# Attention's weighted sums as seven block products, run in 64-column halves of the matmul array

## The chip, the cores and the metric

One core of one Trainium2 chip runs the whole kernel. The metric is the device time of one execution in microseconds (us), lower is better. Engines are named as in the profile: PE (matrix products; PEld loads their stationary operand), DVE (vector), ACT (scalar), POOL (GpSimd) and SP, which only issues transfers (DMAs). ACT and POOL issue transfers too; such an issue takes its place in the engine's own order, so what is written behind it waits until it has been issued.

## The reference

A layer norm, 16-head attention over 2048 rows (head size 128) and a gated feed-forward with ternary weights, all added to x. The change concerns the line that sums `v` with the softmax weights; all of it is float32.

```python
xn = layernorm(x)                                    # x: 1 x 2048 x 256
q, k, v = heads(einsum('bsd,ed->bse', xn, Wqkv))     # 16 heads of 128
logits = einsum('bqhd,bkhd->bhqk', q, k) * 128 ** -0.5
w = softmax(logits)
out = einsum('bhqk,bkhd->bqhd', w, v)                # the weighted sums
x + einsum('bse,de->bsd', out.reshape(1, 2048, 2048), Wout) + ffn(xn)
```

## The kernel before

**Blocks and steps.** After a lead-in of about 100 us (layer norm, feed-forward, first projections) one loop runs over 64 blocks: 16 heads by 4 blocks of 512 queries. Block `n` has four steps, `t` = 0 to 3. A step computes the scores of one tile `v` of 128 queries against all 2048 keys, six tiles ahead of the weighted sums (`LEAD`, L52), and a quarter of the weighted sums of block `n`. So in step `(n, t)` PE works on the scores of tile `u + 6`, DVE turns tile `u + 4` (which is tile `t` of block `n + 1`) and PE sums block `n`.

**A step on each engine.** The loop stands under `tc.manual_schedule()` (L932): each engine runs its instructions in the order in which the code writes them.

- PE: four score products of 512 columns (L612), the first of two "side" products (`beside`; projections of later heads or the output projection, L166, L280 or L783), three or two weighted-sum products (L690), the second side product, the remaining one or two weighted-sum products. Some steps have a single side product or none. Every float32 product of 128 x 128 x 512 appears as two MATMUL records.
- DVE: the two maxima of the scores (L617), their negated maximum `nm` (L620), the sums that read the side products (L186 to L206, L304, L790), the inverses of the softmax sums at `t` = 2 (L660 to L663), the two transposes of an older tile (L680).
- ACT: two exponentials (L627) which need `nm`, then six of the sixteen transfers that exchange 32-row strips between partitions (`exchanged`, L646).
- SP: the other ten of those transfers. An exchange moves `p` into `part`; the transposes L680 then turn `part` into `pT`, with the keys on the partitions. `p` has buffers for two tiles, `part` too.
- POOL: small transfers (`put_away` L708, `spread` L672, the inverses L665, moves of the output sums L716 and L720, `v_exchanged` L311) and differences of operands for the side products (L138 to L141, L261 to L264, L723).

**Buffers in PSUM.** Three score buffers (`ps_s`), one buffer for the weighted sums (`ps_av`, one bank) and one for the side products (`ps_m`).

**Weighted sums.** `weighted(n, k)` adds the product of key tile `k` of `v` (128 keys x 128) and `pT` (128 keys x 512 queries) into one bank, 16 products for a block, four in each step. After the last one a single DVE instruction (L701) multiplies the bank with the inverse softmax sums, which `spread` has laid into `oT`, and `put_away` stores `oT` in DRAM at `t` = 0 of the next block. The last four blocks leave the inverse to a later line; the last block is summed in two halves of 256 columns behind the loop.

**Side products** already use a seven-product scheme for blocks of 2 x 2: differences of operands are formed on POOL, and DVE adds each product into the results that need it.

Of the kernel before, what the change touches and what calls it, by code (L numbers as in the profile page):

```python
# [19 lines left out]
def layernorm_attention_bitffn_kernel(  # L20
# [15 lines left out]
    P = 128  # L36
# [48 lines left out]

    banks = []

    def bank(shape, name: str):
# [63 lines left out]
    def fast_product(h: int, b: int, i: int, second: bool):  # L152

        c = b // 2 * 2
        wk, wq = (weights[h // G, i][:, :, bass.ts(h % G, D)] for i in "kq")
        w, t = ws[h], ts[c]
        x00, x10 = (xnT[:, d, bass.ts(c, QB)] for d in range(KC))
        x11 = xnT[:, 1, bass.ts(c + 1, QB)]
        lhs, rhs = {
            (0, 0): ((wk[:, 0], x00), (w[:, 1], t[:, 1])),  # L160
            (0, 1): ((w[:, 2], t[:, 2]), (wq[:, 1], t[:, 3])),
            (1, 0): ((w[:, 0], t[:, 0]), (w[:, 3], x11)),
            (1, 1): ((wk[:, 1], x10),),
        }[b % 2, i][second]
        pm = ps_m.tile([P, QB], F32, tag="m", name=f"pw{h}_{b}_{i}_{int(second)}")
        nc.tensor.matmul(pm, lhs, rhs, start=True, stop=True)  # L166
        return pm
# [100 lines left out]
    def fast_v_product(g: int, m: int, second: bool):  # L268
# [10 lines left out]
        pm = ps_m.tile([P, QB], F32, tag="m", name=f"pvw{g}_{half}_{m}_{int(second)}")  # L279
        nc.tensor.matmul(pm, lhs, rhs, start=True, stop=True)  # L280
        return pm
# [24 lines left out]
    def v_exchanged(h: int, half: int):  # L306

        v = v_half(h, half).rearrange("p k d -> p (k d)")
        for j in range(P // 32):
            for q in range(P // 32):  # L310
                nc.gpsimd.dma_start(  # L311
                    v_part[q // 2][bass.ts(j, 32), bass.ts(q % 2, S // 8)],
                    v[bass.ts(q, 32), bass.ts(j, S // 8)],
                )
# [284 lines left out]

    def scores(v: int, late=None):  # L600

# [7 lines left out]
        for i in range(2):  # L609
            s = ps_s.tile([P, HALF], F32, tag="s", name=f"s{v}_{i}")  # L610
            for j in range(HALF // QB):
                nc.tensor.matmul(  # L612
                    s[:, bass.ts(j, QB)], qTs[h, b][:, bass.ts(t, P)],
                    kTs[h][:, i * HALF + j * QB : i * HALF + (j + 1) * QB],
                    start=True, stop=True,
                )
            nc.vector.tensor_reduce(mx[:, i : i + 1], s, AX.X, ALU.max)  # L617
            halves.append(s)
        nm = small.tile([P, 1], F32, tag="nm", name=f"nm{v}")
# [49 lines left out]
    def spread(n: int):  # L669

        if n < NBK - NB:
            nc.gpsimd.dma_start(oT, rds[n % 2].rearrange("t p -> (t p)").partition_broadcast(P))  # L672
            rbs[n] = oT

    def transposed(v: int):
        n, t = divmod(v, TB)
        if t == 0:
            pTs[n] = apool.tile([P, TB, NQ, S // NQ], F32, tag="pT", name=f"pT{n}")
        for i, part in enumerate(parts.pop(v)):
            nc.vector.transpose(pTs[n][:, t, 2 * i : 2 * i + 2], part)  # L680

    def weighted(n: int, k: int, part=None):

        h, b = blocks[n]
        t0, t1 = (0, TB) if part is None else (part * TB // 2, (part + 1) * TB // 2)
        if k == 0:
            pool, tag = (ps_s, "s") if part == 0 else (ps_av, "av")
            avs[n] = pool.tile([P, QB], F32, tag=tag, name=f"av{n}_{t0}")
        av = avs[n][:, : (t1 - t0) * P]
        nc.tensor.matmul(  # L690
            av, v_tile(h)[:, v_place(h, k), :],
            pTs[n][:, t0:t1].rearrange("p t g (k q) -> p (t g) k q", q=32)[:, :, k, :],
            start=(k == 0), stop=(k == NKT - 1),
        )
        if k == NKT - 1:

            m = 1 if part == 1 else t1 - t0
            for t in range(t0, t1, m):
                o, a = oT[:, t * P : (t + m) * P], av[:, (t - t0) * P : (t - t0 + m) * P]
                if n < NBK - NB:  # L700
                    nc.vector.tensor_tensor(o, a, rbs[n][:, t * P : (t + m) * P], ALU.mult)  # L701
                else:
                    nc.vector.tensor_copy(o, a)

# [75 lines left out]
    def fast_o_product(g: int, m: int, second: bool):  # L780
        lhs, i, _ = o_parts(g, m)[second]
        pm = ps_m.tile([P, QB], F32, tag="m", name=f"pow{g}_{m}_{int(second)}")
        nc.tensor.matmul(pm, lhs, o3[:, i], start=True, stop=True)  # L783
        return pm
# [47 lines left out]
    def opened(b: int, u: int, pool=ps_m, tag: str = "m"):  # L832

        pm = pool.tile([P, 2, DM], F32, tag=tag, name=f"pp{b}_{u}")
        for j in range(2):
            nc.tensor.matmul(
                pm[:, j], o3[:, b % 2, bass.ts(2 * u + j, P)], weights[H // G - 1, "o"][:, 0, :],
                start=True, stop=True,
            )
# [3 lines left out]
    def projected(n: int, u: int, pool=ps_m, tag: str = "m"):  # L843
# [6 lines left out]
        for j in range(2):  # L850
            t = 2 * u + j
            if j % m == 0:
                pm = pool.tile([P, m, DM], F32, tag=tag, name=f"po{n}_{u}_{j}")
            pms.append(pm[:, j % m, :])
            nc.tensor.matmul(
                pms[j], oT[:, bass.ts(t, P)], weights[H // G - 1, "o"][:, 1, :],
                start=True, stop=True,
            )
# [26 lines left out]
    def between(n: int, t: int):  # L885
# [4 lines left out]
        how = {  # L890
            (5, 0): (v_exchanged, 0, 0), (5, 2): (v_transposed, 0, 0), (6, 1): (v_transposed, 1, 0),
            (7, 0): (v_exchanged, 0, 1), (7, 2): (v_transposed, 0, 1),
        }.get((i, t))
        if t == 0:
            if 0 < n <= last:
                put_away(n - 1)
        if t == 1:
# [16 lines left out]
        if t == 2:  # L914
            if i == GB - 1 and n < last:
                wo = weights[g, "o"]
                sums_of(wo[:, :, :P], wo[:, :, P:], f"wos{g}")
            if i in (5, 7) and g + 1 < H // G:
                v_exchanged((g + 1) * G + 1, i // 2 - 2)
        if t == 3:  # L920
            if i == NB - 1 and g + 1 < H // G:
# [10 lines left out]
    with tc.manual_schedule():  # L932
        for u in range(-LEAD, (NBK - 1) * TB):
# [24 lines left out]
            def beside():  # L958
# [4 lines left out]
                if seven:  # L963
                    pms.append(product(*hi, False))
                    read(*hi, False, pms[0])

            if more:
                scores(v, late=beside)

            if lead_in:  # L970
                for what, hg, i in first.get(v, ()):
                    {"q": q_piece, "k": k_piece, "v": v_piece}[what](hg, i)
                if v == 1:
                    front.close()
                    apool = ctx.enter_context(tc.tile_pool(name="apool", bufs=2))
                    oT = apool.tile([P, QB], F32, tag="oT", name="oT", bufs=1)
                    for c in range(0, NB, 2):
                        x_sums(c)
# [16 lines left out]
            twice = seven and twice  # L995
            ahead = KQ // 2 if first_of_pair else KQ - 1
            if u >= 0:
                for k in range(t * KQ, t * KQ + ahead):
                    weighted(n, k)
            if twice:  # L1000
# [12 lines left out]
            if u >= 0:  # L1013
                for k in range(t * KQ + ahead, (t + 1) * KQ):
                    weighted(n, k)
            if more and t == TB - 1:
# [4 lines left out]
            if t == 2 and n > NBK - NB:  # L1021
                projected(n - 1, 1)
            if u >= 0:
                between(n, t)

        n = NBK - 1
        for k in range(NKT):
            weighted(n, k, 0)
            if k in (KQ - 1, 3 * KQ - 1):
# [3 lines left out]
        for k in range(NKT):  # L1033
            weighted(n, k, 1)
            if k == KQ - 1:
# [41 lines left out]
```

## Time and profile before

| what | value |
|---|---|
| time, median of 3 runs | 2243.78 us (2242.69 to 2244.05) |
| span of the profiled execution | 2242.2 us |
| granted PE clock | 1.000 |
| DVE busy | 1772.0 us (79%) |
| ACT busy (its transfer issues not counted) | 652.4 us (29%) |
| POOL busy (its transfer issues counted) | 681.1 us (30%) |
| transfers of L646: SP, median of one issue | 2556, 589 ns |
| transfers of L646: ACT, median of one issue | 1540, 602 ns |
| DVE transpose of 128 x 256, L814 (nearest to a 256-column DVE sum) | 408 ns |
| ACT copy of 128 x 256 out of PSUM, L235 | 385 ns |
| POOL difference of 128 x 512 / of 128 x 128, L723 / L139 | 1271 / 452 ns |

A timeline line gives the start in us, the length in us, the engine, line and operation, the tiles written and read, the shape and how many instructions were merged; in brackets the idle time before it and what ended it. The engines ACTq and SPq are the issuing of transfers, which the profile doesn't count as busy. A row "x8" of MATMUL records stands for four float32 products. The end of a matmul record is modelled, so the pitch is read from the starts: eight score records started at 1020.28 us and the next record at 1023.71, 0.429 us a record or 0.857 us a product of 512 columns. With 256 columns 24 records of L690 took 5.34 us at the end of the kernel (2232.09 to 2237.43), 0.215 us a record.

### The profile page before, as it was taken

What the parts mean: (1) busy time and instruction counts of PE and PEld (TensorE: products, weight loads), DVE (VectorE), ACT (ScalarE), POOL (GpSimd) and SP (SyncE); (2) the same over time, 40 slices, a digit from 0 to 9 for tenths busy, and PEclk for the clock granted to TensorE, in tenths of its full rate; (3) what the DMA queues carried; (4) which work ended last, traced back from release to release, by engine and by line L of the source; (5) the groups of instructions that cost most, each with busy time, mean ns of one, the idle gap of its engine ahead of it and who ended that gap; (6) DMA issues with size and microseconds to landing.
All of it is one profiled execution on the core that took longest, in us unless ns stands there. A gap on an engine that the chain in (4) does not pass through costs nothing.

```text
span 2242.2 us, 24572 instructions
## 1 busy us (share of the span) xinstructions
PE 2230.5 (99%) x5434; PEld 1025.3 (46%) x5434; DVE 1772.0 (79%) x2329; ACT 652.4 (29%) x1138; POOL 681.1 (30%) x1223
## 2 busy tenths in 40 slices
PE   9999999999999999999999999999999999999999
PEld 6744444444444444444444444444444444444445
DVE  6577778888788878888788878788778887888876
ACT  5543222222222222222222222222222222222231
POOL 0021144231452223522234313332134221452442
PEclk9999999999999999999999999999999999999999
DMA  2166666775676666676666766667566676676775
GB/s 91 50 161 172 156 166 172 186 195 157 165 196 179 185 159 164 188 203 169 155 176 179 197 179 150 176 181 199 163 166 179 175 197 159 158 200 181 197 202 145
DMA packets 252515, 382.72 MB, mean 171 GB/s; under 512 B 86224, under 2 KB 90768, under 8 KB 252368
## 3 DMA queue, kind: packets, MB, share of 16 engines
q1 hardware_dynamic: 127664, 174.95, 30.3%
q10 hardware_dynamic: 74896, 101.94, 17.2%
q0 software_dynamic: 49808, 104.27, 16.6%
q8 instruction: 43, 0.70, 0.1%
q14 instruction: 104, 0.85, 0.1%
HBM read 62.98 MB, written 34.73 MB: 44 GB/s over the span
## 4 chain that ended last, share of the span: by engine, by line
PE 67%; DMA 16%; DVE 7%; SPq 5%; issue 2%; ACTq 2%; ACT 1%; DVEq 0%; POOL 0%
PE s L612 26%; PE av L690 25%; DMA part<-p 16%; PE pw L166 5%; SPq L646 5%; DVE pT L680 3%; PE pvw L280 3%; PE pow L783 3%; PE ph L495 2%; ACTq L646 2%; DVE mx L617 1%; PE pf L518 1%; ACT p L627 1%; DVE osums L790 1%; PE pv L229 1%
## 5 line engine op out<-in xcount | busy, mean ns | idle before, releaser
L627 ACT ACTIVATE p<-s,nm 128x1024 f32<-128x1024 f32 x512 | 566.1, 1110 | 1512.5 <-DMA part<-p 1269.5
L612 PE MATMUL s<-kT,qT 128*128 128x512 f32 x2048 | 922.5, 593 | 2.6 <-ACT p L627 2.4
L617 DVE TENSOR_REDUCE mx<-s 128x1 f32<-128x1024 f32 x512 | 623.6, 1221 | 353.5 <-PE s L612 353.3
L690 PE MATMUL av<-pT,v 128*128 128x512 f32 (+1 forms) x1952 | 888.4, 585 | 0.0
L680 DVE STREAM_TRANSPOSE pT<-part 128x1024 f32<-128x1024 f32 x512 | 605.2, 1220 | 37.3 <-DMA part<-p 31.1
L612 PEld LDWEIGHTS s<-kT,qT 128*128 128x128 f32 x2048 | 388.3, 190 | 493.6 <-issue 474.7
L690 PEld LDWEIGHTS av<-pT,v 128*128 128x128 f32 x1952 | 370.9, 190 | 450.2 <-issue 448.0
L665 POOL DMA_DIRECT2D rd<-r x240 | 124.9, 527 | 616.8 <-DVE r L663 614.0
L311 POOL DMA_DIRECT2D xnT<-v x448 | 221.1, 501 | 84.9 <-DVE v L304 54.4
L723 POOL TENSOR_TENSOR o<-o 128x512 f32<-128x512 f32 x56 | 71.2, 1271 | 198.6 <-PE pow L783 168.4
L708 POOL DMA_DIRECT2D od<-oT x60 | 34.1, 568 | 300.5 <-DVE oT L701 300.5
L790 DVE TENSOR_TENSOR osums<-pow,osums 128x512 f32<-128x512 f32 x196 | 124.2, 675 | 0.0
L627 ACT ACTIVATION_READ_ACCUMULATOR p<-s,nm 128x1 f32 x512 | 100.3, 196 | 0.0
L166 PE MATMUL pw<-t,ws 128*128 128x512 f32 x168 | 86.6, 597 | 1.0 <-DVE kT L193 1.0
L189 DVE TENSOR_TENSOR kT<-pw,kT 128x512 f32<-128x512 f32 x112 | 74.7, 667 | 0.0
L304 DVE TENSOR_TENSOR v<-pvw,v 128x512 f32<-128x512 f32 x98 | 65.5, 680 | 0.1
L690 PE MATMUL av<-pT,osums 128*128 128x512 f32 x128 | 59.5, 592 | 0.0
L186 DVE SCALAR_TENSOR_TENSOR qT<-pw,qT 128x512 f32<-128x512 f32 x84 | 57.5, 684 | 0.1
L166 PE MATMUL pw<-xnT,wk 128*128 128x512 f32 x112 | 57.2, 592 | 0.0
L783 PE MATMUL pow<-o,wos 128*128 128x512 f32 x112 | 57.2, 592 | 0.0
L166 PEld LDWEIGHTS pw<-t,ws 128*128 128x128 f32 x168 | 31.0, 189 | 44.1 <-issue 34.0
L620 DVE TENSOR_REDUCE nm<-mx 128x1 f32<-128x2 f32 x256 | 39.7, 155 | 13.4
(140 smaller groups left out, 1146.6 us busy)
## 6 DMA issues: line engine op xcount, KB each, us to landing
part<-p SPq DMA_DIRECT2D x2556, 64.0 KB, 2.2
part<-p ACTq DMA_DIRECT2D x1540, 64.0 KB, 2.5
oT<-rd POOLq DMA_DIRECT2D x60, 256.0 KB, 4.1
od<-oT POOLq DMA_DIRECT2D x60, 256.0 KB, 3.3
o<-od POOLq DMA_DIRECT2D x60, 256.0 KB, 4.5
xnT<-v POOLq DMA_DIRECT2D x448, 32.0 KB, 2.4
osums<-yd POOLq DMA_DIRECT2D x28, 512.0 KB, 5.4
yd<-osums POOLq DMA_DIRECT2D x28, 512.0 KB, 4.7
```

What stands on the lines that cost most here:

```text
L166: nc.tensor.matmul(pm, lhs, rhs, start=True, stop=True)
L189: nc.vector.tensor_tensor(k, pk, base, ALU.add)
L311: nc.gpsimd.dma_start(v_part[q // 2][bass.ts(j, 32), bass.ts(q % 2, S // 8)], v[bass.ts(q, 32), bass.ts(j, S // 8)],)
L612: nc.tensor.matmul(s[:, bass.ts(j, QB)], qTs[h, b][:, bass.ts(t, P)], kTs[h][:, i * HALF + j * QB : i * HALF + (j + 1) * QB], start=True, ...
L617: nc.vector.tensor_reduce(mx[:, i : i + 1], s, AX.X, ALU.max)
L627: nc.scalar.activation(p, s, AF.Exp, bias=nm, accum_out=sums[n][:, t, i : i + 1],)
L646: queue.dma_start(parts[v][g // 2][bass.ts(j, 32), g % 2, :], ps[j // 2][bass.ts(g, 32), bass.ts(j % 2, S // NQ)],)
L665: nc.gpsimd.dma_start(rds[n % 2][:, bass.ts(j, 32)], riT[32 * j : 32 * j + TB, :])
L680: nc.vector.transpose(pTs[n][:, t, 2 * i : 2 * i + 2], part)
L690: nc.tensor.matmul(av, v_tile(h)[:, v_place(h, k), :], pTs[n][:, t0:t1].rearrange("p t g (k q) -> p (t g) k q", q=32)[:, :, k, :], start=( ...
L783: nc.tensor.matmul(pm, lhs, o3[:, i], start=True, stop=True)
L790: nc.vector.tensor_tensor(y, pm, y, ALU.add)
```

## The change

**Seven products.** A block's sum is a product of `v` turned (128 x 2048) and the turned weights (2048 x 512). Both are cut in two each way: `v` into halves of its 128 columns and of the keys (`l11`, `l12`, `l21`, `l22`, each 1024 keys x 64), the weights into halves of the queries and of the keys (four slots of 128 x 2048 values in the new tile `R`). Seven products of such blocks replace eight. `R` has seven slots, whose roles `(a, b, c, d, e)` rotate from block to block (`roles`); the transposes write `a, b` at `t` = 0, 1 and `c, d` at `t` = 2, 3.

**Column halves.** A product with 64 stationary columns uses half of the array; `weighted(n, r, k)` issues two of them, one for each half, with different moving operands of 256 columns. The four rounds `r` = 0 to 3 of a block run in steps `t` = 0 to 3 and have 8, 8, 8 and 4 such pairs (`units`); the seventh product is shared by the two halves. All other products of the loop are split by `in_halves` into two of 64 columns with the same moving operand.

**Differences on POOL.** For each block four differences of whole slots, `T1` to `T4`; `T1`, `T2` and `T3` in two instructions each (128 x 1024), `T4` in one (128 x 2048). For each head four sums or differences of parts of `v` (128 x 512, `v_combined`).

**Putting the products together.** The results of a round are spread over the halves of the bank. `copied(m, r)` on ACT copies a 64 x 256 part into the SBUF tile `u` (one copy after rounds 0 and 3, two after round 1), `added(m, r)` on DVE adds another part to it (one sum after rounds 0 and 3, two after round 2). `copied` stands at the head of the next step, before its scores, so on ACT behind the six transfers of the tile before; the sums after rounds 3 and 0 stand between the two maxima of the next step, those of round 2 before them. After round 3 DVE multiplies `u` with the inverses into `oT`. The bank is still single.

**Moves.** `put_away` comes later in step `t` = 0; half of the 16 transfers of `v_exchanged` go to SP, and the calls are one step later.

```diff
+    def in_halves(out, lhs, rhs, start, stop, both=(True, True)):
+        for c in range(2):
+            if both[c]:
+                nc.tensor.matmul(
+                    out[c * HP : (c + 1) * HP], lhs[:, c * HP : (c + 1) * HP], rhs,
+                    start=start, stop=stop, skip_group_check=True,
+                )
...
-                nc.gpsimd.dma_start(
+                queue = nc.sync if q % 2 else nc.gpsimd
+                queue.dma_start(
...
             nc.vector.tensor_reduce(mx[:, i : i + 1], s, AX.X, ALU.max)
+            if i == 0 and between_maxes:
+                between_maxes()
...
     def transposed(v: int):
         n, t = divmod(v, TB)
+        lo, hi = roles[n][t // 2 * 2 : t // 2 * 2 + 2]
         for i, part in enumerate(parts.pop(v)):
-            nc.vector.transpose(pTs[n][:, t, 2 * i : 2 * i + 2], part)
+            to = R[:, lo : hi + 1 : hi - lo].rearrange("p s (t g c) -> p t g s c", t=2, g=NQ)
+            nc.vector.transpose(
+                to[:, t % 2, 2 * i : 2 * i + 2],
+                part.rearrange("p g (s c) -> p g s c", s=2),
+            )
...
+        o, x, y = {"T1": (e, c, a), "T2": (a, d, e), "T3": (c, d, c), "T4": (b, b, a)}[todo]
...
+        nc.gpsimd.tensor_tensor(o, x, y, ALU.subtract)
...
+    def weighted(n: int, r: int, k: int):
...
+        todo = (
+            ((0, l12, b, first), (0, l11, a, first)),
+            ((1, st[:, 0], e, first), (0, st[:, 1], a, False)),
+            ((1, st[:, 2], d, False), (0, s3, c, False)),
+            ((0, l22, b, first), (0, l22, b, False)),
+        )[r]
+        for i, (half, l, s, start) in enumerate(todo):
+            kk = k2 if i == 0 else k
+            nc.tensor.matmul(
+                av[i * HP : (i + 1) * HP, half], l[:, kk], moving(s, kk),
+                start=start, stop=(k == units[r] - 1), skip_group_check=True,
+            )
...
+    def copied(n: int, r: int):
...
+        todo = (
+            ((lo, q0, hi, 0),), ((hi, q1, lo, 1), (lo, q1, hi, 0)), (), ((hi, q0, lo, 0),),
+        )[r]
+        for op, oq, ap, half in todo:
+            nc.scalar.copy(u[op, oq], av[ap, half])
+
+    def added(n: int, r: int):
...
+        todo = (((lo, q0, 0),), (), ((lo, q1, 1), (hi, q1, 0)), ((hi, q0, 0),))[r]
+        for p, q, half in todo:
+            nc.vector.tensor_tensor(u[p, q], av[p, half], u[p, q], ALU.add)
+        if r == 3 and n < NBK - NB:
+            nc.vector.tensor_tensor(oT, u, rbs[n], ALU.mult)
...
+            m, r = (n, t - 1) if t else (n - 1, 3)
+            if m >= 0:
+                copied(m, r)
+                if r == 2:
+                    added(m, r)
+
+            def sums_so_far():
+                if m >= 0 and r != 2:
+                    added(m, r)
+
+            if t == 0 and n >= 0:
+                differences(n, "T1b")
...
             if more:
-                scores(v, late=beside)
+                scores(v, late=beside, between_maxes=sums_so_far)
...
-            ahead = KQ // 2 if first_of_pair else KQ - 1
+            ahead = units[t] // 2 if first_of_pair else units[t] * 3 // 4
             if u >= 0:
-                for k in range(t * KQ, t * KQ + ahead):
-                    weighted(n, k)
+                for k in range(ahead):
+                    weighted(n, t, k)
```

## The prediction

> **What bounds it now.** I read the busy times first, then the groups, then the timeline of one block.
>
> ```profile
> PE 2230.5 (99%) x5434; PEld 1025.3 (46%) x5434; DVE 1772.0 (79%) x2329; ACT 652.4 (29%) x1138; POOL 681.1 (30%) x1223
> ...
> L627 ACT ACTIVATE p<-s,nm 128x1024 f32<-128x1024 f32 x512 | 566.1, 1110 | 1512.5 <-DMA part<-p 1269.5
> L612 PE MATMUL s<-kT,qT 128*128 128x512 f32 x2048 | 922.5, 593 | 2.6 <-ACT p L627 2.4
> ...
> L690 PE MATMUL av<-pT,v 128*128 128x512 f32 (+1 forms) x1952 | 888.4, 585 | 0.0
> ```
>
> PE is the bound and hardly ever waits: 2.6 us before all scores, nothing before the weighted sums. So work taken from PE shows in full, and so does every new wait of PE. ACT looks idle (29%), but its idle time ends with its own transfers. The timeline shows why, at a passage from t = 3 (scores from 1020.28) to t = 0 (from 1028.86):
>
> ```profile
> 1020.28 3.60 PE L612 MATMUL s<-kT,qT 128*128 128x512 f32 x8
> ...
> 1023.91 1.22 DVE L617 TENSOR_REDUCE mx<-s 128x1 f32<-128x1024 f32 x1 [0.49 <-PE s L612]
> ...
> 1025.17 0.15 DVE L620 TENSOR_REDUCE nm<-mx 128x1 f32<-128x2 f32 x1
> ...
> 1025.41 1.11 ACT L627 ACTIVATE p<-s,nm 128x1024 f32<-128x1024 f32 x1 [5.70 <-DVE nm L620]
> ...
> 1026.51 1.10 ACT L627 ACTIVATE p<-s,nm 128x1024 f32<-128x1024 f32 x1
> ...
> 1027.74 4.50 ACTq L646 DMA_DIRECT2D part<-p  x6
> ...
> 1028.86 3.60 PE L612 MATMUL s<-kT,qT 128*128 128x512 f32 x8
> ...
> 1032.29 1.02 PE L783 MATMUL pow<-o,wos 128*128 128x512 f32 x2
> 1033.15 2.74 PE L690 MATMUL av<-pT,v 128*128 128x512 f32 x6
> ```
>
> The exponentials start 5.13 us after their scores, and ACT is free only when its six issues end: 11.96 us after the scores, 3.38 us into the next step. The weighted sums begin 4.29 us into that step. Nothing on PE waits for ACT's tail today. The change hangs PE on it.
>
> An undisturbed tail is shorter; this one ends 6.07 us after its exponential began (858.26 to 864.33), against 6.83 above:
>
> ```profile
> 858.26 1.11 ACT L627 ACTIVATE p<-s,nm 128x1024 f32<-128x1024 f32 x1 [6.21 <-DMA part<-p]
> ...
> 860.59 3.74 ACTq L646 DMA_DIRECT2D part<-p  x6
> ```
>
> **PE's gain.** A block's sums are 16 products of 0.857 = 13.72 us. After: 28 pairs of 64-column products over 256 columns. A record of 256 columns takes 0.215 us, a float32 product two. If the two halves of a pair run side by side, a pair takes 0.429 us and the block 12.01: 1.71 us less, all of it in t = 3 (8 pairs become 4), 108 us for 63 blocks. The last block keeps its work. No row shows halves side by side. The other end is one after the other: then all products of the loop take twice as long, about +2000 us. I take side by side: the halves occupy different columns and write different partitions, and loading is no obstacle (128 columns in 190 ns are hidden behind a record of 0.215 us today). The other end stands as a rival.
>
> The Trainium skill (TensorE: Matmul & The Clock Gate, "Part 3: Packing small matmuls") gives 2.38 times for three column tiles, side by side then; no row here can confirm it for float32.
>
> **ACT's copies, the new wait.** Round r + 1 accumulates on the part that `copied(r)` reads, and the single bank cannot be opened for a new block before `copied` and `added` of round 3 are through. I also let the products wait for the sums after round 0, which read the same bank. `copied` is queued on ACT behind the six issues. Behind the waiting sum on DVE stand the second maximum, `nm`, and so the exponentials, whose tail delays the next copy. Prices: copy 0.38 (L235), sum 0.41 (L814's 256 columns), multiplication 0.69 (L701), maximum 1.22, `nm` 0.15; hand-overs 0.05 to 0.1 each. For ACT's tail, from exponential to last issue, the two rows give 6.07 and 6.83; I take 6.3, nearer the undisturbed one, as longer steps spread the same transfers. A block, all times from the start of its step's scores:
>
> - t = 3 lasts 6.87 (scores 3.43, four pairs 1.72, two side products 1.71), or 6.01 with one side product, in half the blocks. ACT ends at 5.13 + 6.3 - 6.87 = 4.56 into t = 0. Copy, sum and hand-overs: PE may go on at 5.50 instead of 4.29, a stall of 1.21 (or 2.07): mean 1.64. The multiplication and second maximum follow, so the exponentials start at 7.6 (8.45) instead of 5.13, and the step lasts 9.79 (10.65).
> - t = 1: ACT ends at 7.6 + 6.3 - 9.79 = 4.11; copy and sum to 5.05; stall 0.76. Exponentials at 6.5; the step lasts 9.34, or 8.48 with one side product.
> - t = 2: ACT ends at 3.43 (4.29), two copies to 4.29 (5.15): stall 0 or 0.86, mean 0.43. At t = 3 ACT has no copy and is on time again.
>
> Sum 2.83 us a block against 1.71 gained: +1.12 x 62 = **+69 us**. With 6.07 the stalls are 2.1, +24 us; with 6.83 they are about 4.6 (three waits, 3.26 us per us of tail), +179 us.
>
> **POOL.** 128 x 512 takes 1.271 and 128 x 128 0.452, so 2.13 ns a column and 0.18 fixed: 2.36 for 1024 columns, 4.54 for 2048. A block gets 6 x 2.36 + 4.54 = 18.7 us and a quarter of four 1.27: 20.0. It has 681.1 / 64 = 10.6, less 224 issues of 0.50 moved to SP (1.75 a block): 28.9 of some 34.6 us. T2 must follow round 0 and be ready for round 1: its second half starts at the end of t = 0, takes 2.36, is due 4.3 into t = 1 at the earliest. That holds except behind the eighth block of a group, whose own POOL work (sums, moves, eight issues) makes 36: some 3 us late, seven times. I take 0; bounds 0 and +25. `put_away`, now ahead of T2's first half in POOL's order, waits for the multiplication (6.2 into t = 0); T2 waits for four pairs of round 0 anyway (5.50 + 1.72), so it costs nothing.
>
> **DVE** gains four sums and has the multiplication for L701: 27.7 + 1.6 = 29.3 of 34.6 us, hidden as long as blocks are longer than 30. The new multiplication reads SBUF twice. No row of before shows that beside a POOL difference; with one SBUF input four of L790 took 2.48 us beside L723 (at 1008.93), no more than elsewhere. The Trainium skill (SBUF — State Buffer, "Who interferes with whom") speaks against the change here: such an instruction and a GpSimd instruction that reads SBUF exclude each other for a whole instruction. By that rule the multiplication would wait up to 1.3 us behind the sums of `v` once in each head, an estimate of +10 to +20 us.
>
> **SP** gets eight issues of 0.59, 4.7 us, in 28 steps of the run beside its ten (5.9). The exchange is needed two steps later; bounds 0 and, if exponentials slip by 2, +56. I take 0.
>
> **Sum.** 2242.2 + 69 = 2311; the median of runs stands 1.6 above the span: **2313 us**. This case's own range: 2255 to 2430.
>
> **Rivals.**
>
> - *PE keeps its stream, faster.* The copies come before 4.3 in most steps: if ACT's issues shorten as steps are rearranged, or the sums are not waited for. For: the shortest tail misses the mark by under a microsecond at t = 0 with two side products. Against: at t = 3 the step shrinks by just the 1.71 us that would have covered it. Without a stall 2244 - 108 = 2136; it turns faster where stalls stay under 1.71 a block; middle 2190. 21%.
> - *Gain and stall cancel*: within 0.2% (4.5 us, about what this measurement can tell from no change). 5%.
> - *POOL is the bound*, slower still: its block of 28.9 us has forced waits (T1 for the transposes, T2 for round 0, the inverses), and if differences run a fifth longer beside DVE, 20 becomes 24 and a block 36 to 38: 2400 to 2530. It decides once POOL's work and waits pass 34.6. 4%.
> - *The halves do not overlap*: about 4200. 5%.
>
> The main case has 65%; slower in all 74%, same 5%, faster 21%. The range 2190 to 2440 leaves out some 10% below and 10% above.
>
> **What would show it.** PE's idle time before the first pair of rounds 0, 1, 2, released by ACT's copies or DVE's sums, about 1.6, 0.8 and 0.4 us; the score records at 0.429 us per two halves; exponentials at 7 to 8 us after their scores at t = 0; no idle PE at t = 3. Wrong would be: PE still at 99% (then faster), POOL without gaps and PE released by differences, or score records at twice the pitch.

## The result and the profile after

The changed kernel takes **2577.21 us** (median of four, 2567.18 to 2585.45) against 2243.91 (2242.69 to 2246.77) for the kernel before on the same chip: **1.1483 times the time, interval 1.1451 to 1.1515**. The forecast was 2313 us, 2190 to 2440. The direction and the kind of loss were right, the size was not: the loss is 333 us, not 69.

The profiled execution's span is 2578.8 us. Its page, the engines, the granted clock and the groups around the weighted sums (L776 sums, L794 copies, L802 sums on DVE, L804 the multiplication, L729 the differences):

```profile
PE 2252.7 (87%) x13386; PEld 1096.7 (43%) x13386; DVE 1941.5 (75%) x2578; ACT 745.3 (29%) x1390; POOL 1824.1 (71%) x1504
...
PEclk9999999999999999999999999999999999999888
...
L729 POOL TENSOR_TENSOR R<-R 128x1024 f32<-128x1024 f32 x441 | 1175.4, 2672 | 233.5 <-PE av L776 125.7
L93 PE MATMUL s<-kT,qT 128*64 128x512 f32 x4000 | 910.3, 595 | 0.2 <-ACT p L643 0.2
...
L776 PE MATMUL av<-R,v 128*64 128x256 f32 x3728 | 607.7, 409 | 133.6 <-DVE oU L802 133.1
...
L776 PE MATMUL av<-R,st 128*64 128x256 f32 x3024 | 495.6, 391 | 107.2 <-ACT oU L794 76.0
...
L794 ACT COPY oU<-av 64x256 f32<-64x256 f32 x248 | 91.2, 368 | 883.2 <-DMA part<-p 757.2
```

The last column is the idle time just before the group and what ended it. The weighted sums, which waited 0.0 us, now wait 240.8; the scores still wait for nothing. The waits are ended by DVE's sums and ACT's copies, and the copies' own idle time ends with `part<-p`, ACT's transfers of the tile before. That is the chain forecast. No engine is full: PE fell from 99% to 87%, POOL rose from 30% to 71%.

The same passage as a timeline, a step t = 0 whose scores start at 1300.26, and then t = 2:

```profile
1300.68 4.12 ACTq L662 DMA_DIRECT2D part<-p  x6
...
1304.84 0.36 ACT L794 COPY oU<-av 64x256 f32<-64x256 f32 x1 [4.19 <-DMA part<-p]
1305.24 0.43 DVE L802 TENSOR_TENSOR oU<-av,oU 64x256 f32<-64x256 f32 x1 [1.82 <-ACT oU L794]
...
1305.72 2.81 PE L776 MATMUL av<-R,v 128*64 128x256 f32 x24 [1.00 <-DVE oU L802]
1306.42 1.23 DVE L631 TENSOR_REDUCE mx<-s 128x1 f32<-128x1024 f32 x1
...
1323.38 4.55 POOL L729 TENSOR_TENSOR R<-R 128x2048 f32<-128x2048 f32 x1
1323.42 0.75 ACT L794 COPY oU<-av 64x256 f32<-64x256 f32 x2 [4.61 <-DMA part<-p]
...
1324.22 0.43 PE L776 MATMUL av<-R,st 128*64 128x256 f32 x1 [1.00 <-ACT oU L794]
1324.23 0.43 PE L776 MATMUL av<-R,v 128*64 128x256 f32 x1
...
1324.49 0.38 PE L776 MATMUL av<-R,st 128*64 128x256 f32 x1
...
1324.50 0.38 PE L776 MATMUL av<-R,v 128*64 128x256 f32 x1
...
1324.92 3.03 DVE L676 TENSOR_TENSOR r<-sum 128x4 f32<-128x4 f32 x1
```

Three things are to be seen. The copy starts when the sixth issue ends (1300.68 + 4.12), the sum follows, PE follows the sum, and the second maximum stands behind the sum. The two halves of a pair start 0.01 us apart (1324.49 and 1324.50) and the next pair 0.21 later: they run side by side. And a sum of 128 x 4 values on DVE, 0.15 us in the kernel before, takes 3.03 us and ends as the difference on POOL ends (1323.38 + 4.55 = 1327.93, 1324.92 + 3.03 = 1327.95).

A fourth stands in the windows. The columns are length; busy time and instruction count of PE, PEld, DVE, ACT and POOL; granted clock; DMA share and GB/s. Below them the same stretch in PE's timeline:

```profile
1336.00:1339.00 3.00, 3.00 (x16) 0.84 (x12) 3.00 (x5) 1.25 (x4) 2.35 (x2) 1.00 0.54 127
1339.00:1342.00 3.00, 0.07 (x2) 0.00 (x0) 1.03 (x1) 0.00 (x0) 2.96 (x7) 0.99 0.79 185
1342.00:1348.60 6.60, 5.39 (x24) 2.66 (x24) 6.03 (x5) 0.62 (x2) 6.48 (x7) 0.50 0.55 146
1349.00:1355.00 6.00, 5.29 (x30) 2.59 (x32) 4.53 (x5) 1.64 (x4) 5.98 (x5) 1.00 0.61 177
```

```profile
1342.95 5.39 PE L776 MATMUL av<-R,v 128*64 128x256 f32 x24 [3.88 <-DVE oU L802]
```

After 3.88 us of idle PE the clock is granted at 0.50, and the 24 half products that took 2.81 us at 1305.72 take 5.39. So a long wait is paid for twice.

**Where the 333 us are**, by the records of the loop: PE is idle for 321 us (7 before). Ahead of the weighted sums 122.5 us at t = 0 (behind DVE's sums), 70.6 at t = 2 (behind ACT's copies), 27.5 at t = 1 and 15.6 at t = 3, together 236; the other 85 are mostly second side products that wait until DVE has read the first. The clock stood at half for 184.6 us, in which PE was busy for 156, so some 78 us are lost. With the gain of 108 that was forecast, 314 + 78 - 108 = 284; the last 49 us are not told apart (records just after a gap are longer, which is part of it).

### The profile page after: what moved, and what is told of

Same layout as the page of the kernel before. It is cut to its first block, busy times and chain, and to the rows that moved or that the text cites. A ratio compares the mean times of both kernels' runs of the same rounds, so it can differ in the third digit from the quotient of the medians.

```text
span 2578.8 us, 41888 instructions
## 1 busy us (share of the span) xinstructions
PE 2252.7 (87%) x13386; PEld 1096.7 (43%) x13386; DVE 1941.5 (75%) x2578; ACT 745.3 (29%) x1390; POOL 1824.1 (71%) x1504
## 5 line engine op out<-in xcount | busy, mean ns | idle before, releaser
L729 POOL TENSOR_TENSOR R<-R 128x1024 f32<-128x1024 f32 x441 | 1175.4, 2672 | 233.5 <-PE av L776 125.7
L93 PE MATMUL s<-kT,qT 128*64 128x512 f32 x4000 | 910.3, 595 | 0.2 <-ACT p L643 0.2
L776 PE MATMUL av<-R,v 128*64 128x256 f32 x3728 | 607.7, 409 | 133.6 <-DVE oU L802 133.1
L709 DVE STREAM_TRANSPOSE R<-part 128x1024 f32<-128x1024 f32 x512 | 605.2, 1221 | 50.5 <-POOL R L729 38.1
L776 PE MATMUL av<-R,st 128*64 128x256 f32 x3024 | 495.6, 391 | 107.2 <-ACT oU L794 76.0
L93 PEld LDWEIGHTS s<-kT,qT 128*64 128x64 f32 x4000 | 314.6, 138 | 446.8 <-issue 410.1
L776 PEld LDWEIGHTS av<-R,v 128*64 128x64 f32 x3728 | 345.7, 147 | 350.5 <-DVE oU L802 165.9
L776 PEld LDWEIGHTS av<-R,st 128*64 128x64 f32 x3024 | 303.1, 140 | 353.1 <-issue 132.7
L794 ACT COPY oU<-av 64x256 f32<-64x256 f32 x248 | 91.2, 368 | 883.2 <-DMA part<-p 757.2
L802 DVE TENSOR_TENSOR oU<-av,oU 64x256 f32<-64x256 f32 x248 | 104.0, 420 | 224.0 <-ACT oU L794 207.9
L322 POOL DMA_DIRECT2D xnT<-v x224 | 111.6, 505 | 31.4 <-DVE v L330 28.7
L804 DVE TENSOR_TENSOR oT<-oU,oT 128x512 f32<-128x512 f32 x60 | 83.3, 1388 | 2.1
```

The costliest lines, as they stand in the source:

```text
L93: nc.tensor.matmul(out[c * HP : (c + 1) * HP], lhs[:, c * HP : (c + 1) * HP], rhs, start=start, stop=stop, skip_group_check=True,)
L322: queue.dma_start(v_part[q // 2][bass.ts(j, 32), bass.ts(q % 2, S // 8)], v[bass.ts(q, 32), bass.ts(j, S // 8)],)
L709: nc.vector.transpose(to[:, t % 2, 2 * i : 2 * i + 2], part.rearrange("p g (s c) -> p g s c", s=2),)
L729: nc.gpsimd.tensor_tensor(o, x, y, ALU.subtract)
L776: nc.tensor.matmul(av[i * HP : (i + 1) * HP, half], l[:, kk], moving(s, kk), start=start, stop=(k == units[r] - 1), skip_group_check=True,)
L794: nc.scalar.copy(u[op, oq], av[ap, half])
```

## The experiments

Two theories first: **A**, PE waits for copies and sums that are queued behind ACT's six issues; **B**, POOL's differences, their load and DVE held beside them. Two more could be seen at once: **C**, halves are slower; **E**, `v`'s exchange, half of it moved to SP, comes late. Ratios are to the kernel before, run beside each; "copies first" is the base of all later runs.

### Halves alone

The kernel before with all its loop's products as two halves of 64 columns; one of the places:

```diff
-        nc.tensor.matmul(pm, lhs, rhs, start=True, stop=True)
+        in_halves(pm, lhs, rhs, True, True)
```

> The kernel before with all loop products split into two of 64 columns, nothing else. Theory A (the loss is waits of PE: copies and sums queued behind ACT's six issues) and theory B (the loss is DVE and POOL excluding each other): the halves run side by side, 2244 us within 10, PE busy 99%. Theory C (half products are slower by themselves): PE is busy 130 us longer in the changed kernel than its product count asks for, so 2300 to 2375 us.

Measured 2245.2 us, 1.0011 [1.0002, 1.0021].

```profile
PE 2229.6 (99%) x10362; PEld 910.8 (41%) x10362; DVE 1773.1 (79%) x2329; ACT 652.3 (29%) x1138; POOL 681.3 (30%) x1223
```

Twice the instructions of the loop in the same PE time: C falls. That halves run side by side, which the forecast could not see in any row, is shown.

### One cause at a time in the changed kernel

ACT's six issues of a step move behind the copies at the head of the next step:

```diff
+            if queue is nc.scalar:
+                late_issues.append(move)
...
             if m >= 0:
                 copied(m, r)
+            exchanged_late()
```

> The changed kernel with ACT's six issues of a tile written behind the copies of the next step instead of ahead of them. Theory A: the copy runs some 0.5 us after the round's end, PE's idle time in front of rounds 0 to 2 falls from about 250 us to under 60, clock near 1.0, time 2180 to 2300 us. Theory B: DVE's stalls beside POOL (76 us) and POOL's load stay and decide, time above 2450 us. Theory C: PE's busy time stays 130 us too long, 2270 to 2400 us.

DVE's instructions with two SBUF inputs go: the multiplication to POOL, the sum of the two halves of the softmax sums as a reduction of one operand:

```diff
-            nc.vector.tensor_tensor(oT, u, rbs[n], ALU.mult)
+            nc.gpsimd.tensor_tensor(oT, u, rbs[n], ALU.mult)
-        nc.vector.tensor_tensor(ri[:, :TB], sums[n][:, :, 0], sums[n][:, :, 1], ALU.add)
+        nc.vector.tensor_reduce(ri[:, :TB], sums[n], AX.X, ALU.add)
```

> The changed kernel with the multiplication by the inverses on POOL and the softmax sums added by a reduction with one SBUF input, so that DVE has no such instruction with two SBUF inputs beside POOL. Theory A: DVE's 58 us of stalls go, most of them inside waits that stay: 2520 to 2577 us, PE's idle time still above 220 us. Theory B: 2300 to 2450 us, PE's idle time under 180 us.

The differences are made for the first block alone; those of the 62 later ones are left out:

```diff
     def differences(n: int, what: str):
+        if n:
+            return
```

> The changed kernel with the four differences T1 to T4 formed for the first block alone, so POOL loses 18.7 us a block (the sums are then those of unmodified slots). Theory A: the waits on copies and sums stay, 2450 to 2577 us, PE idle above 200 us. Theory B: POOL is out of the way, 2150 to 2350 us.

All of `v`'s issues go back to POOL, at the steps of the kernel before:

```diff
-                queue = nc.sync if q % 2 else nc.gpsimd
+                queue = nc.gpsimd
```

> The changed kernel with the exchanges of v all on POOL and at the steps of the kernel before. Theory A alone: the waits on copies decide everywhere, 2550 to 2600 us. Theory E (SP's eight extra issues hold back the exchange of p, and the late exchange of v holds back DVE and POOL behind the eighth block): 2470 to 2530 us, the blocks after the eighth (44.1 us in the changed kernel) at 39 us or less.

| run | us | ratio, interval |
|---|---|---|
| copies_first | 2390.8 | 1.0665 [1.0647, 1.0682] |
| no_two_inputs | 2531.0 | 1.1287 [1.1259, 1.1314] |
| differences_once | 2519.5 | 1.1235 [1.1189, 1.1282] |
| v_as_before | 2632.3 | 1.1735 [1.1711, 1.1758] |

**A is the largest cause**: the order of two kinds of instruction on ACT is worth 186 us. The groups of copies_first show it:

```profile
L787 PE MATMUL av<-R,v 128*64 128x256 f32 x3728 | 576.4, 394 | 93.8 <-DVE oU L813 93.2 <-DVE oT L813 0.4
L787 PE MATMUL av<-R,st 128*64 128x256 f32 x3024 | 479.9, 380 | 14.9 <-POOL R L740 11.3 <-ACT oU L805 1.8 <-DVE oU L813 1.5
...
L805 ACT COPY oU<-av 64x256 f32<-64x256 f32 x248 | 91.1, 367 | 109.3 <-PE av L787 106.4
```

The copies now wait for PE (106.4) and not for `part<-p` (757.2 before this edit), and the products that waited 76.0 for copies wait 1.8. B in its plain form falls short: all differences away are worth 58 us, the two kinds of DVE instruction taken out 46. E falls: putting `v` back makes it 55 slower. But A is not the whole: PE's waits ahead of rounds 0 to 2 fell to 45 us, as expected, yet 49 remain ahead of round 3, where the changed kernel had 16, and copies_first lies above A's own range (2180 to 2300 us), 6.7% above the kernel before.

### What keeps copies_first up

Three combinations of the edits above: copies first and one SBUF input; copies first and `v` as before; all three.

> The last two edits together: ACT's six issues behind the copies, and no DVE instruction with two SBUF inputs beside POOL. With the copies ahead 2391 us were measured; in that profile DVE loses 56 us to such instructions and steps t = 3 are 1.7 us longer than their products, behind DVE. Theory A with exclusion as a second cause: 2300 to 2360 us, t = 3 back under 7.2 us. If DVE's delay at t = 3 has another cause (the exchange lands later): 2375 to 2400 us.

> ACT's six issues behind the copies and the exchanges of v as before. With the copies ahead the first block of a group still takes 46.3 us, 14 more than its products. Theory E: that block falls under 38 us, time 2310 to 2350 us. Theory B (POOL's load is what delays that block; the edit gives POOL 224 issues back): no gain, 2385 to 2430 us.

> All three edits. If the causes found are all there are, the time comes near the product count: 2180 to 2260 us, PE idle under 90 us. If POOL's 75% load with its forced waits is a bound by itself: 2290 to 2360 us.

They gave 2399.8 (1.0696 [1.0680, 1.0712]), 2472.6 (1.1024 [1.1008, 1.1041]) and 2478.3 us (1.1048 [1.1029, 1.1066]): 9, 82 and 88 us *slower* than copies_first; for all three together 2360 or less had been expected. Taking out the two SBUF inputs gains nothing more here. Giving `v` back had been expected to gain or to change nothing, and 82 us for eight issues that change their queue, and come a step earlier, called for a look at what is in that queue. In copies_first most blocks last 31 to 35 us between their first scores, but the first block of a group of eight 46.3 and the seventh 37.6, just behind steps that exchange `v`; the third lasts 36.9. The turn of a group:

```profile
959.50 7.57 SPq L322 DMA_DIRECT2D xnT<-v  x8
...
967.17 7.79 SPq L671 DMA_DIRECT2D part<-p  x12
968.58 1.30 DVE L330 STREAM_TRANSPOSE v<-xnT 128x512 f32<-128x512 f32 x2 [2.54 <-DMA xnT<-v]
...
971.03 0.43 DVE L813 TENSOR_TENSOR oU<-av,oU 64x256 f32<-64x256 f32 x1
...
971.51 4.11 PE L787 MATMUL av<-R,v 128*64 128x256 f32 x18 [5.09 <-DVE oU L813]
```

SP issues eight transfers of `v` among its ten of `p`; DVE stands in `v`'s transposes for 2.54 us, the sum of the round before is behind them, and PE waits 5.09 us for that sum. Two runs move the issues: copies_v_later puts the second head's two exchanges into the next group, copies_spread spreads them, in pieces, over several steps. (In copies_v_later the last group's moved exchange shares its buffer with the moves of the output sums, so that one head's sums there are others.) A third has copies first and the differences of the first block only. The edit shown is from copies_spread.

```diff
+        (7, 1): (0, 1, (0, 1, 2, 3)), (7, 3): (0, 1),
+        (8, 2): (1, 1, (0,)), (8, 3): (1, 1, (1,)), (9, 0): (1, 1, (2,)), (9, 1): (1, 1, (3,)),
+        (9, 3): (1, 1),
...
-            if i in (5, 7) and g + 1 < H // G:
-                v_exchanged((g + 1) * G + 1, i // 2 - 2)
```

> copies_first with the second head's two v exchanges moved from steps (5,3) and (7,3) of a group to steps (2,1) and (3,1) of the next group, their transposes to (2,3) and (3,3), where that head is not yet read. If the leftover is a crowd of issues at the turn of a group (block 0 of a group 46.3 us, block 6 37.6, the others 31 to 35), these two fall to 33 to 35 and the time to 2390.8 - 7 x 12 to 15, some 2285 to 2310. If the crowd only moves with the issues, blocks 2 and 3 grow by what 0 and 6 lose: 2370 to 2400.

> copies_first with the same transfers of v in other places: the first head's second half is issued at step (7,1) ahead of that step's exchange of p (in copies_first its eight SP issues stand behind it and start 12 us later), the other three halves in pieces of four or eight issues over two to four steps, the second head's second half at steps (0,2) to (1,1) of the next group with its transposes at (1,3). If the leftover comes from eight SP issues standing in one place among the ten of p, so that DVE's transposes wait for xnT<-v and part<-p and PE for DVE, blocks 0 and 6 of a group fall from 46.3 and 37.6 to 34 to 38 and the time to 2270 to 2320. If it is the number of issues that counts and not their place, the delay is only shared out: 2370 to 2420. If POOL's differences hold what is left, the first block stays above 42 and the time above 2350.

> copies_first (2390.8) with the differences T1 to T4 made for the first block of the run alone; the later blocks' differences are left out, so POOL loses some 19 us a block and the output is not the sum wanted. If what copies_first still loses sits in POOL (its load, DVE excluded beside it, products waiting for R), PE keeps its stream and the time falls to 2140 to 2220, below the kernel before. If it sits in the queues and waits of ACT, SP and DVE by themselves, at most the 58 us that the same edit gave to the changed kernel go: 2330 to 2390.

| run | us | ratio, interval | blocks 0, 2, 6, 7 of a group, us (mean of the second to the seventh group) |
|---|---|---|---|
| copies_first | 2390.8 | 1.0665 [1.0647, 1.0682] | 46.3, 36.9, 37.6, 31.5 |
| copies_v_later | 2461.2 | 1.0966 [1.0938, 1.0994] | 41.7, 41.0, 38.2, 31.5 |
| copies_spread | 2399.5 | 1.0689 [1.0670, 1.0707] | 43.3, 42.7, 33.0, 33.7 |
| copies_once | 2338.4 | 1.0423 [1.0387, 1.0459] | 44.3, 37.8, 35.5, 34.0 |

Moved issues take their delay with them; copies_v_later took longer than either of its ranges. There block 0 falls from 46.3 to 41.7, and blocks 2, 3 and 4 rise from 36.9, 32.2 and 34.7 to 41.0, 35.4 and 38.9. In copies_spread block 6 falls from 37.6 to 33.0, but block 0 only to 43.3, and block 2 rises to 42.7: the place of the eight issues alone is not the cause, while their number and POOL's differences both remain possible by that run's expectation. And without differences block 0 stays slow (44.3), as `v` still stands on SP. So two edits remained that had been made only one at a time: copies_once_v leaves out the later differences *and* gives `v` back to POOL; copies_no_v keeps the differences and leaves out `v`'s exchange (its transposes read old data); the edit shown is the latter's, the former joins two that are shown above (with `v` on POOL its issues also come a step earlier).

```diff
     def v_exchanged(h: int, half: int):
+        return
```

> copies_first with two edits at once: the differences made for the first block only (those of later blocks are left out) and v's sixteen issues all on POOL at the steps of the kernel before. Either edit alone left the time high (2338.4 and 2472.6). If the rest is one cause, POOL's 19 us of differences that crowd v's issues either in POOL or, moved, into SP's exchange of p, then with both undone PE keeps its stream in nearly all steps: 2150 to 2210, under the kernel before. If ACT's copies and DVE's sums alone still make PE wait, 2260 to 2330.

> copies_first with v's exchange left out (the transposes of v then read old data): eight SP and eight POOL issues less, four times in a group; differences, copies and sums stay. If the crowd of v's issues is the whole of what copies_first loses, blocks 0 and 6 of a group fall to 33 and the time to 2200 to 2260. If DVE held beside POOL's differences is most of it, only DVE's short waits for v go: 2320 to 2380.

They gave **2219.2 us, 0.9896 [0.9867, 0.9924]** (2150 to 2210 expected), and 2294.5 us, 1.0224 [1.0207, 1.0241]. The page of copies_once_v:

```profile
PE 2154.4 (97%) x13386; PEld 1112.3 (50%) x13386; DVE 1867.5 (84%) x2578; ACT 744.4 (34%) x1390; POOL 779.8 (35%) x1294
...
PE   9999999999999999999999999999999999999898
...
PEclk9999999999999999999999999999999999999999
```

From copies_first, the differences away alone give 52 us, `v` to POOL alone costs 82, the two together give 172. So the same move of `v` costs 82 beside the differences and gains 119 without them (2338.4 to 2219.2): **the differences fill POOL, and `v`'s issues then have no queue that is free.** On POOL they stand among the differences, on SP among the ten issues of `p`. With both undone all blocks of a group last 31.2 to 34.7 us and PE is busy in every slice. But this kernel does less than it should.

The differences cost something without `v` too: copies_no_v fell between its two ranges, and with no exchange at all it is 75 us above copies_once_v, which has one. About half of that can be named. copies_one_input took two kinds of DVE instruction away from POOL's side and left a third, the scaling of `qT` (L222, a single SBUF input); one group and one wait of copies_first:

```profile
L222 DVE TENSOR_SCALAR qT<-kT 128x512 f32<-128x512 f32 x28 | 62.7, 2238 | 1.0
...
PE pw L93 <- DVE qT L196: 37.5, 27, 1.6
```

It takes 2238 ns instead of 427, 27 of 28 times beside a difference (L740), and stands on DVE ahead of the sums of `qT` for which PE then waits: 37.5 us, 39.2 in copies_one_input, 38.4 in copies_no_v and 0.5 in copies_once_v, where it takes 427 ns. So DVE held beside POOL is not done with; no run took this instruction away, and the link is read from the order on DVE alone.

### Seven products in some blocks only

To keep the result and part the two causes, some blocks of each group of eight were given the eight products again (no differences, no copies, one multiplication from `av`), all with the copies first: blocks 0, 4, 5, 6 with `v` on SP and POOL; blocks 0, 5, 6, 7 or 0, 4, 5 with `v` on POOL.

```diff
+        if plain(n):
+            nc.tensor.matmul(
+                av[:, r // 2], v_tile(h)[:, v_place(h, k + r % 2 * KH), :], moving((a, b, c, d)[r], k),
+                start=(r % 2 == 0 and k == 0), stop=(r % 2 == 1 and k == KH - 1), skip_group_check=True,
+            )
+            return
```

In plain_0567 POOL also gives back the quarter of `v` that `v_combined` has overwritten, once in each second head:

```diff
+                    nc.gpsimd.tensor_tensor(l21, l11, l21, ALU.subtract)
```

> copies_first with blocks 0, 4, 5 and 6 of each group of eight by the eight products of the kernel before (full columns, no differences, no copies, one multiplication from av), and 1, 2, 3 and 7 by seven. If what copies_first loses comes from POOL's differences and v's issues meeting in blocks 0 and 6, those blocks fall from 46.3 and 37.6 to 34 to 36, and the four others keep their 31.5 to 33.7: some 2225 to 2260, about the kernel before or under it. If the loss is in the seven products' copies and sums as such, half of it stays: 2300 to 2330.

> copies_v (copies first, v's issues on POOL at the steps of before) with blocks 0, 5, 6 and 7 of each group by eight products, 1 to 4 by seven, and one subtraction a head on POOL that gives back v's overwritten quarter. v's 64 issues then meet almost no differences. If the two together are the cause, the slow blocks of copies_v (46.1, 36.4, 39.3, 37.7) fall to 33 to 35, the seven-product blocks stand at 31.5 to 34: 2215 to 2245. If not: 2300 or more.

> copies_v with blocks 0, 4 and 5 by eight products and 1, 2, 3, 6 and 7 by seven: v's issues of steps (7,0) and (7,3) meet the differences, those of (5,0) and (5,3) do not. By the theory of the two together, blocks 6 and 7 stay slow (36 to 39) and block 5 falls to 33: 2260 to 2300, between plain_0567 and copies_v.

They gave 2411.5 (1.0740 [1.0724, 1.0756]), 2338.7 (1.0418 [1.0403, 1.0434]) and 2401.7 us (1.0709 [1.0690, 1.0727]), all far above what was expected. Part of it was waits: in plain_0456_sp, with half of `v`'s issues on SP, block 0 still lasts 42.5 us though it has no differences (36.0 in plain_0567); in plain_045 blocks 6 and 7 stay slow (40.6, 37.6), as expected. The other part was of my own making: a step of an eight-product block lasted 9.30 us with no wait in it. In plain_0567, the step whose scores start at 1504.17:

```profile
1504.17 3.65 PE L93 MATMUL s<-kT,qT 128*64 128x512 f32 x16
1507.65 1.03 PE L93 MATMUL pow<-o,wos 128*64 128x512 f32 x4
1508.61 2.86 PE L790 MATMUL av<-R,v 128*128 128x256 f32 x12
1511.40 1.08 PE L93 MATMUL pow<-o,wos 128*64 128x512 f32 x4
1512.40 1.13 PE L790 MATMUL av<-R,v 128*128 128x256 f32 x4
1513.47 3.65 PE L93 MATMUL s<-kT,qT 128*64 128x512 f32 x16
```

Sixteen records should take 16 x 0.215 = 3.44 us, and the step 8.6. I took the full-column product over 256 columns to be slower, by 0.7 / 16 = 0.044 us a record. The rows say otherwise: twelve records take 2.79 us to the start of the next product (1508.61 to 1511.40) and four take 1.07 (1512.40 to 1513.47), so a record costs (2.79 - 1.07) / 8 = 0.215 as before, and 0.21 us is lost once in each run of them; the side products ahead of the two runs take 0.96 and 1.00 us to the next start instead of 0.86. The time is lost where products of 64 and of 128 columns change: 0.35 us for each run of full-column products among halves, two runs in this step; steps with one run last 8.09, so 0.35 over 7.74. The mend is the same: these products were issued as two halves as well (four_plain, blocks 0, 5, 6, 7), and in five_plain block 2 went back to eight products too:

```diff
-            nc.tensor.matmul(
-                av[:, r // 2], v_tile(h)[:, v_place(h, k + r % 2 * KH), :], moving((a, b, c, d)[r], k),
+            in_halves(
+                av[:, r // 2], v_tile(h)[:, v_place(h, k + r % 2 * KH), :], moving((a, b, c, d)[r], k),
...
```

> plain_0567 with each of its eight-product sums issued as two halves of 64 columns, not as one of 128 columns over 256. In plain_0567 the steps of those blocks last 9.30 and 8.09 us where 8.6 and 7.74 were expected, so a 128-column product over 256 columns costs some 0.04 us more than its 0.215. If the load of 128 columns is what shows there, the halves give back 0.7 us a step, 32 blocks x 2.6: 2245 to 2260, and any waits left are in blocks 2 and 6. If not, 2330 to 2345.

> four_plain with block 2 of a group by eight products as well (one combination of v more a head): seven products in blocks 1, 3 and 4 only. By the theory that waits come where differences, v's issues and a block's own POOL and DVE work meet, block 2 falls from 36 to 34 and PE hardly waits: 2215 to 2240, under the kernel before. If the seven products lose by themselves, it stands above 2244.

four_plain took 2280.3 us, 1.0157 [1.0143, 1.0171], five_plain 2264.1, **1.0085 [1.0071, 1.0099]**. The steps of the eight-product blocks are back at 8.60; 58 us came back, some 25 less than expected. Counted by runs (201 in plain_0567's trace, 0.35 us each) 70 were to come back, not 83. The seven-product blocks of five_plain last 32.0, 32.0 and 33.3 us, where the same blocks of halves_alone last 33.6, 33.7 and 34.3. It still loses, in the last eight blocks: windows from the first scores of block 56 to the end, of five_plain and then of halves_alone:

```profile
1991.40:2263.40 272.00, 235.88 (x1607) 127.65 (x1602) 188.58 (x253) 64.18 (x116) 153.57 (x167) 0.95 0.60 162
```

```profile
2001.80:2241.80 240.00, 233.12 (x1206) 91.71 (x1202) 179.41 (x242) 60.82 (x106) 85.70 (x136) 1.00 0.68 183
```

Up to there five_plain is 10 us ahead; then it loses 32, with PE waiting for 36 us instead of 7 and a clock of 0.95. There the moves of the output stand on POOL beside the differences, which may be the cause and was not tested. With eight products in the last group as well, some 2232 us are to be had by these two rows, an estimate that was not run. No kernel that computes everything was faster than the kernel before.

## Why the prediction was wrong in size

- **PE's gain of 1.71 us a block, halves side by side: right.** Halves alone cost 0.1%, and a step t = 3 with one side product lasts 6.02 us where it is not disturbed (forecast 6.01). In the calm blocks of copies_once_v some 1.4 us of the 1.71 arrive (31.24 against 32.62).
- **The wait for ACT's tail: right in kind, too small.** Forecast were stalls of 1.64, 0.76 and 0.43 us at t = 0, 1, 2; the trace has 122.5, 27.5 and 70.6 us over 62 blocks, so 1.98, 0.44 and 1.14, and 0.25 at t = 3: 236 us instead of 175. The tail was mis-sized: the mean from exponential to last issue is 6.7 us at t = 0 and 3, 7.5 at t = 1 and 8.3 at t = 2, not 6.3; over the loop of the kernel before it was already 7.0 to 7.4, above both rows that I read. The undisturbed row that I took as the nearer one is not what steps with waits look like; with the other row, 6.83, the working gave +179 us. The exponentials of t = 0 start 9.3 us after their scores in the mean, where 7 to 8 were to be seen. copies_first shows what the order on ACT is worth, with the clock lost behind its waits: 186 us.
- **"Hidden as long as blocks are longer than 30" failed for DVE.** Its time was summed, and its place in the chain was not asked. DVE's sum releases PE, so what delays DVE delays PE. The multiplication takes 1388 ns in the mean (L804), twice the 0.69 of L701, and a held instruction ends as POOL's ends (1327.95 and 1327.93 us). The Trainium skill (SBUF — State Buffer, "Who interferes with whom") states that the two exclude each other. The estimate of +10 to +20 us priced only the multiplication behind the four sums of `v` in each head, not the seven instructions of differences in every block, and no other DVE instruction. Over the changed kernel DVE loses some 76 us in this way: 42 in the multiplication (19 of 60 are held), 22 in the sums of the softmax sums (L676, L671), 12 in the scaling L222. no_two_inputs is 46 faster.
- **POOL 0 and SP 0: both failed, and they belong together.** Each was costed alone, POOL by its total (28.9 of 34.6 us fit) and SP by its number of issues. Both fit; what did not fit was `v`'s issues beside the one or the other. From copies_first 96 us go without `v`'s exchange and 172 with differences and SP's share both undone.
- **No term for the clock.** The forecast took PE's rate as given. Half the clock after gaps costs some 78 us, and it makes the loss grow faster than the waits.
- **Waits elsewhere.** Side products that wait for DVE were not in the sum; with them 78 us of idle time stand outside the weighted sums that before did not.

So the step that failed is the row of terms that the sum put at nothing (DVE hidden, POOL 0, SP 0, no clock), and the tail was too short. Together: 61 us more before the weighted sums, 78 elsewhere on PE, 78 of clock; of the 264 us between forecast and result 47 are not told apart. Of the rivals, "POOL is the bound" was not it, though the time lay near its range: POOL is 71% busy, and without its differences the kernel still took 2519.5 us.

## What to carry over

A queue that is hardly busy can still have no room: ask of each new instruction what stands ahead of it in its engine's order, transfers included, and who waits for it. Put the short instruction on which the bound engine waits ahead of the issues that nobody waits for; here that order alone was worth 186 us. And cost moved work by pairs: two moves that fit one at a time may have no place left when both are made.

## What was not expected of the hardware

- **PE's clock.** In the changed kernel all 16 gaps of over 3.5 us after the lead-in were followed by a granted clock of 0.50, 23 of 44 between 2 and 3.5 us, 1 of 28 between 1.5 and 2, none of 28 between 0.8 and 1.5. The slow stretches last 3.4 us or a multiple in nearly all cases. The Trainium skill (TensorE: Matmul & The Clock Gate, "What's actually happening") tells of idle windows of about 3.4 us that halve the clock; the trace agrees in length, and shows that gaps of 2 to 3 us are often enough. Which ones is to be read from the trace: all 41 slow stretches start on one grid of 3.413 us. Four windows of that grid, in the columns of above:

```profile
1338.48:1341.90 3.42, 0.58 (x4) 0.00 (x0) 1.55 (x2) 0.00 (x0) 3.23 (x7) 1.00 0.81 189
1341.90:1345.31 3.41, 2.36 (x12) 1.41 (x14) 2.81 (x2) 0.36 (x1) 3.39 (x4) 0.50 0.68 194
1345.31:1348.72 3.41, 3.03 (x16) 1.25 (x12) 3.34 (x4) 0.38 (x1) 3.31 (x4) 0.50 0.41 98
1348.72:1352.14 3.42, 2.43 (x16) 1.44 (x18) 3.42 (x5) 1.92 (x4) 3.42 (x3) 1.00 0.46 143
```

  A window's clock follows PE's busy share in the window before it: 0.58 of 3.42 us brings 0.50, 2.36 of 3.41 keeps it there, 3.03 of 3.41 brings 1.00 back. In the loops of the changed kernel, copies_first and v_as_before, the clock fell 100 times: behind every window with PE busy under 40%, behind none over 43%. From half clock it came back behind no window busy up to 78% and behind every one from 79%, as this profile counts busy.
- **Two float32 halves of 64 columns** with different moving operands and 256 columns start within 0.01 us of each other (in other places within 0.04) and keep a pitch of 0.215 us a pair of records. Full-column products over 256 columns keep 0.215 a record too, but each run of them among halves costs 0.35 us once.
- **A DVE instruction with one SBUF input** can be held too: L222, 128 x 512 by a scalar, took 0.43 us before (L212), 0.86 in the mean in the changed kernel (6 of 28 were held) and 2.24 in copies_first.
